# First two pairs of row tiles by eight block products, position by position, in a float32 conv + LoRA kernel

## Chip, core and metric

One NeuronCore of a Trainium2 chip. The metric is the device time of one launch in microseconds (us). Engines: PE (TensorE, matmul), ACT (ScalarE), DVE (VectorE), POOL (GpSimd), SP (SyncE, which here only issues loads). Every engine works through its own queue of instructions in order; semaphores make one wait for another.

## The reference

```
x        (64, 64, 1024)   64 samples, 64 channels, length 1024
v = grouped conv1d(x, weight (64,16,9), 4 groups, pad 4) + cond @ c_weight.T + bias    # per sample, channel
W        (1024, 1024), bias (1024,)                       # of the dense layer, on the last axis
A_eff[b] = sum_n gate[b,n] lora_A[n]   (32, 1024)         # 8 blocks b of 8 samples
B_eff[b] = sum_n gate[b,n] lora_B[n]   (1024, 32)
y = v @ W + bias + (v @ A_eff.T) @ B_eff.T + (v @ A_shared.T) @ B_shared.T
out = x + y
```

All arrays are float32.

## The kernel before

**Tiles.** 64 samples x 64 channels are 4096 rows. A row tile has 128 rows, a pair p has two, and there are 16 pairs. Two pairs share one block b of the LoRA tables.

**Arithmetic.** A float32 operand is split into a high part (cast to float32r by ACT, `hi_of`, L236) and a low part (the difference, on DVE or POOL, `lo_of`, L241); a product is high x high + high x low + low x high, so three matmuls of 128x128 by 128x512 for each of four positions k of a block, twelve for a block product.

**Steps of a pair.** `xload p g` loads a quarter of the pair's input; `xhi`, `xlo` split it; `conv p g` runs six matmuls (L274) into one of two PSUM banks for it; `evac` adds the condition on the way to SBUF (DVE, or ACT in four pieces); `turned` transposes on DVE (L293). Groups 0 and 1 make up the first row tile, 2 and 3 the second. The pair's activations are then a 2x2 block matrix A11, A12, A21, A22 (row tile x half of the inner axis), W is B11, B12, B21, B22.

**Products.** Each pair is multiplied by seven block products (Winograd's form of Strassen's method), with sums of A blocks (`asum`: S1 to S4, on POOL, L316) and of W blocks (`wsum`: T1, T3, N4, T2, L385):

```
PRODUCTS = ((A11, B11, "a"), (A12, B21, "a"), (S1, T1, "d"), (S3, T3, "c"), (A22, N4, "c"), (S2, T2, "b"), (S4, B22, "d"))
```

`prod p j` is product j of pair p (L490). `yhi`, `ylo` split its A operand. `keep` copies an accumulator to SBUF (ACT, L537), `xsum`, `ysum`, `radd`, `yadd` form the sums of products that the method asks for and add them to the residual rows (DVE, some on POOL, L543 to L560). `lora p b` makes the small product with the LoRA A table (L501, L502), `delta` adds the product with the B table and the bias to the accumulators (L566), `total` adds an accumulator to the residual rows (DVE, L572), `store` writes them. Five PSUM banks (`pmm`) serve products, `fmm`, `mix`, `cmul` and separate deltas.

**Weights.** W comes as 16 pieces of 128x512 (`wload k h`, two DMAs each). The shared LoRA is folded into it: `fmm k h` multiplies (L375), `fadd k h` adds the result to the piece (DVE, L379). `whi b k` and `wlo b k` split a piece, in place b for a block or a sum of blocks. All pieces lie in one pool of 57 slots. The gated LoRA tables are made in the kernel: `lload` loads 16 pieces (256 KB each), `mix` multiplies by the gates (L424), `mixout` copies out (ACT), `mixput` writes to DRAM, and per block b `aload`, `ahi`, `adiff`, `alo` and `bload`, `bhi`, `blo` fetch and split what is needed. `saload`, `sahi`, `salo`, `sbload`, `sbhi`, `sblo` do it for the shared tables.

**Order.** A single hand-written string, `ORDER`, names all steps; each step issues its instructions, and at the end dependencies without semaphores fix that order within each engine. A letter v, p or a at a step's end names DVE, POOL or ACT. `busy n` runs n matmuls on constants at the start. Before, the first two pairs interleave products with single positions: `prod p j k 1 alone` is position k of product j, and with alone = 1 it goes to an accumulator of its own ("e"), added by another `total`. Products of pairs 0 and 1 run there in the order 3, 5, 6, 2, 4, 0, 1, each for both pairs, as the sums of W become ready.

Of the kernel before, what the change touches and what calls it, by code (L numbers as in the profile page):

```python
# [15 lines left out]
P = 128  # L16
# [21 lines left out]
A11, A12, S1, S3, A22, S2, S4 = range(7)  # L38
# [3 lines left out]

BLOCKS = ("a", "d", "c", "b")

ORDER = """
warm, twload 0, gload, small 1, busy 26, saload 0, twload 1, small 0, xload 0 0, cwload, ctload, xload 0 1,
xload 0 2, thi 0, xload 0 3, sbload 0, bihi, tlo 0 v, saload 1, sbload 1, bilo, thi 1, wload 4 1, tlo 1 v,
wload 0 1, xhi 0 0, cwide, wload 5 1, xhi 0 1, xlo 0 0 v, cmul, wload 1 1, xlo 0 1 v, conv 0 0, wload 6 1,
csum, wload 2 1, sahi 0, salo 0 p, sbhi 0, conv 0 1, xload 1 2, evac 0 0 v, sahi 1, xload 1 0, sblo 0 v,
xload 1 1, sbhi 1, wload 7 1, turned 0 0, salo 1 p, evac 0 1 a, wload 3 1, sblo 1 v, wload 0 0, xhi 0 2,  # L50
turned 0 1, fmm 4 1, fmm 0 1, xhi 0 3, wload 1 0, fmm 5 1, fadd 0 1, xlo 0 2 p, fmm 1 1, fmm 6 1, wload 2 0,
fadd 4 1, fmm 2 1, wload 3 0, conv 0 2, fadd 6 1, xlo 0 3 p, xload 1 3, fadd 2 1, biput 0, fmm 7 1, biput 1,
fadd 5 1, wsum 3 0 p, evac 0 2 a, fmm 3 1, rload 0 1, conv 0 3, rload 1 1, fadd 1 1, xhi 1 0, turned 0 2,
fmm 0 0, whi 3 0, fmm 1 0, fmm 2 0, xlo 1 0 v, evac 0 3 a, fadd 7 1, wlo 3 0 p, xload 2 0, conv 1 0, xhi 1 1,
turned 0 3, xlo 1 1 v, wsum 3 1 p, lload 0 0, fmm 3 0, xhi 1 2, fadd 1 0, xload 2 1, conv 1 1, evac 1 0 a,
asum 0 3, fadd 0 0, whi 3 1, wload 4 0, fadd 2 0, fmm 4 0, fmm 5 0, yhi 0 3, fadd 3 0, xlo 1 2 p, fmm 6 0,
xhi 1 3, ylo 0 3 v, fmm 7 0, evac 1 1 a, conv 1 2, xlo 1 3 v, wlo 3 1 p, lload 0 1, wload 5 0, fadd 3 1, gmask,
conv 1 3, xhi 2 0, turned 1 0, wsum 3 2 p, wload 6 0, prod 0 3 0 1 0, evac 1 2 v, whi 3 2, wload 7 0,
turned 1 1, xlo 2 0 p, prod 0 3 1 1 0, xhi 2 1, turned 1 2, evac 1 3 a, xload 2 2, conv 2 0, fadd 4 0,
wlo 3 2 p, lload 0 2, wsum 3 3 v, mix 0 0, evac 2 0 a, fadd 6 0, xlo 2 1 p, prod 0 3 2 1 0, fadd 5 0, whi 3 3,  # L60
lload 0 3, xload 2 3, mix 0 1, fadd 7 0, mixout 0 0, wlo 3 3 p, lload 0 4, lload 0 5, conv 2 1, lload 0 6,
xhi 2 2, turned 1 3, lload 0 7, mixout 0 1, lload 1 0, xlo 2 2 v, asum 1 3, lload 1 1, prod 0 3 3 1 0,
mixput 0 0, wsum 2 0 v, evac 2 1 a, mixput 0 1, mix 0 2, lload 1 2, wsum 5 0 v, asum 0 2, xload 3 0, yhi 1 3,
mix 0 3, whi 5 0, lload 1 3, ylo 1 3 v, mix 0 4, keep 0 3, wlo 5 0 v, wsum 2 1 p, mixout 0 3, prod 1 3 0 1 0,
mixout 0 4, mixput 0 3, asum 0 5, wsum 5 1 v, mix 0 5, lload 1 4, mixout 0 2, mixput 0 4, mix 0 6, whi 5 1,
mixput 0 2, asum 0 6, yhi 0 5, wlo 5 1 v, prod 1 3 1 1 0, mixout 0 5, ylo 0 5 v, mix 0 7, yhi 0 6, mixput 0 5,
wsum 2 2 v, asum 1 2, prod 1 3 2 1 0, mixout 0 6, ylo 0 6 v, prod 0 5 0 1 0, mixout 0 7, mixput 0 6,
wsum 5 2 v, lload 1 5, asum 1 5, xhi 2 3, prod 1 3 3 1 0, mixput 0 7, whi 5 2, xlo 2 3 v, prod 0 5 1 1 0,
keep 1 3, asum 1 6, wlo 5 2 v, xload 3 1, conv 2 2, yhi 1 5, wsum 2 3 v, whi 6 0, ylo 1 5 v, wsum 5 3 p,
prod 0 5 2 1 0, yhi 1 6, wlo 6 0 v, lload 1 6, prod 1 5 0 1 0, xhi 3 0, aload 0, ylo 1 6 v, conv 2 3, asum 0 2,  # L70
whi 5 3, xlo 3 0 v, wlo 5 3 v, whi 6 1, xload 3 2, prod 1 5 1 1 0, wlo 6 1 p, xhi 3 1, lload 1 7,
prod 0 5 3 1 0, whi 6 2, xlo 3 1 v, prod 1 5 2 1 0, asum 1 2, wlo 6 2 v, whi 6 3, xload 3 3, keep 0 5,
prod 0 6 0 1 1, wlo 6 3 v, yhi 0 2, prod 1 5 3 1 0, wsum 4 0 v, wsum 4 1 p, whi 2 0, prod 0 6 1 1 1, ylo 0 2 v,
keep 1 5, prod 1 6 0 1 1, wlo 2 0 v, wsum 4 2 p, yhi 1 2, mix 1 0, adiff 0 v, ahi 0, ylo 1 2 v, prod 1 6 1 1 1,
whi 2 1, alo 0 v, mixout 1 0, prod 0 6 2 1 1, wlo 2 1 v, wsum 4 3 p, aload 1, whi 2 2, mixput 1 0, mix 1 1,
wlo 2 2 v, whi 2 3, prod 1 6 2 1 1, mixout 1 1, wlo 2 3 v, lora 0 2, whi 4 0, mixput 1 1, mix 1 2, wlo 4 0 v,
whi 4 1, adiff 1 p, prod 0 6 3 1 1, wlo 4 1 v, whi 4 2, mixout 1 2, prod 1 6 3 1 1, wlo 4 2 v, yhi 0 4,
mixput 1 2, mix 1 3, total 0 1 1, whi 4 3, mix 1 4, total 1 1 1, ylo 0 4 p, yhi 1 4, wlo 4 3 v, whi 0 0,
prod 0 2 0 1 0, ylo 1 4 v, mixout 1 3, lora 0 3, prod 0 2 1 1 0, mixout 1 4, wlo 0 0 v, mixput 1 3, whi 0 1,
mixput 1 4, mix 1 5, turned 2 0, wlo 0 1 v, whi 0 2, prod 1 4 0 1 0, mixout 1 5, turned 2 1, wlo 0 2 p,  # L80
prod 0 2 2 1 0, evac 2 2 a, mixput 1 5, evac 2 3 v, prod 0 4 0 1 0, whi 0 3, turned 2 2, mix 1 6, wlo 0 3 v,
whi 1 0, mix 1 7, mixout 1 6, wlo 1 0 v, prod 0 4 1 1 0, whi 1 1, mixput 1 6, turned 2 3, mixout 1 7,
prod 1 2 0 1 0, wlo 1 1 v, asum 2 2, mixput 1 7, prod 0 4 2 1 0, whi 1 2, prod 1 2 1 1 0, asum 2 3,
prod 0 4 3 1 0, wlo 1 2 v, prod 1 2 2 1 0, whi 1 3, bload 0 0, yhi 0 0, lora 1 2, wlo 1 3 v, prod 1 2 3 1 0,
ylo 0 0 v, bload 0 1, lora 1 3, yhi 1 0, total 1 1, prod 0 0 0 1 0, rload 0 2, ysumd 1, ylo 1 0 p,
prod 0 2 3 1 0, rload 0 3, prod 0 0 1 1 0, yhi 0 1, total 0 1, prod 1 0 0 1 0, bhi 0 0, ylo 0 1 v,
prod 0 0 2 1 0, bhi 0 1, ysumd 0, blo 0 0 p, prod 1 0 1 1 0, total 0 2, prod 0 0 3 1 0, rload 1 2, blo 0 1 v,
yadd 0 p, prod 1 0 2 1 0, xsum 0 5, rload 1 3, lora 0 0, radd 0 1 v, radd 0 2 p, prod 1 0 3 1 0, yhi 1 1,
radd 0 3 v, prod 0 1 0 1 0, ylo 1 1 v, lora 0 1, prod 0 1 1 1 0, xsum 1 5, axlow 0, conv 3 0, yadd 1 v,
radd 1 1 p, axsum 0, radd 1 3 v, axhi 0, prod 0 1 2 1 0, axlo 0, xhi 3 2, prod 1 1 0 1 0, evac 3 0 v,  # L90
prod 0 1 3 1 0, xlo 3 2 v, prod 1 1 1 1 0, yhi 2 0, turned 3 0, xload 4 0, delta 0 1 1, ylo 2 0 v, delta 0 2 1,
delta 0 0 0, lora 1 0, total 0 1 2, prod 1 1 2 1 0, yhi 2 1, total 0 2 2, delta 0 3 1, store 0 1, lora 1 1,
ylo 2 1 v, store 0 2, prod 1 1 3 1 0, ahi 1, total 0 3 2, prod 2 0, axlow 1, alo 1 v, store 0 3, yhi 2 2,
aload 2, ylo 2 2 v, rload 0 0, rload 1 0, lora 2 0, keep 2 0, prod 1 4 1 1 0, axsum 1, yhi 2 3, bload 1 0,
prod 2 1, adiff 2 v, axhi 1, ylo 2 3 v, total 0 0 0, asum 2 5, axlo 1, store 0 0, asum 2 6, prod 1 4 2 1 0,
delta 1 1 1, prod 1 4 3 1 0, total 1 1 2, delta 1 2 1, yhi 2 4, total 1 2, delta 1 3 1, delta 1 0 0, bload 1 1,
lora 2 1, store 1 1, bhi 1 0, total 1 3 2, ylo 2 4 p, conv 3 1, yhi 2 5, radd 1 2 v, store 1 3, total 1 0 0,
blo 1 0 p, prod 2 2, xhi 3 3, total 1 2 2, store 1 0, evac 3 1 a, rload 2 0, xlo 3 3 v, ylo 2 5 p, xload 4 1,
store 1 2, turned 3 1, bhi 1 1, rload 2 2, blo 1 1 v, lora 2 2, rload 2 1, keep 2 2, conv 3 2, rload 2 3,
yhi 2 6, rload 3 0, ylo 2 6 v, prod 2 3, xhi 4 0, evac 3 2 v, xlo 4 0 v, rload 3 2, turned 3 2, xload 4 2,  # L100
conv 3 3, yhi 3 0, keep 2 3, ylo 3 0 v, lora 2 3, ysum 2 v, xhi 4 1, prod 2 4, axlow 2, evac 3 3 v, xlo 4 1 p,
axsum 2, turned 3 3, axhi 2, xload 4 3, axlo 2, asum 3 2, prod 2 5, yhi 3 1, ylo 3 1 v, asum 3 3, delta 2 0,
yhi 3 2, xsum 2, prod 2 6, total 2 0, ylo 3 2 p, radd 2 2 v, store 2 0, radd 2 1 v, radd 2 3 p, delta 2 2,
yhi 3 3, prod 3 0, total 2 2, yadd 2 v, ylo 3 3 p, store 2 2, rload 3 1, asum 3 5, delta 2 1, keep 3 0,
lora 3 0, total 2 1, asum 3 6, delta 2 3, yhi 3 4, conv 4 0, total 2 3, rload 3 3, store 2 1, ylo 3 4 v,
store 2 3, prod 3 1, xhi 4 2, evac 4 0 v, xlo 4 2 v, turned 4 0, xload 5 0, lora 3 1, bload 2 0, conv 4 1,
yhi 3 5, bload 2 1, ylo 3 5 v, prod 3 2, xhi 4 3, evac 4 1 v, xlo 4 3 v, turned 4 1, xload 5 1, lora 3 2,
# [112 lines left out]
def adaln_ffn(ctx: ExitStack, tc: tile.TileContext, xt, x, tw, w0, w1, w2, la, lb, gt,  # L220
# [488 lines left out]
```

## Time and profile before

| | us |
|---|---|
| median of 3 runs | 510.44 (510.01 to 510.85) |
| profiled execution, its own time | 510.2 |
| its span, first to last instruction | 508.2 |
| PE busy | 489.5 (96%) |
| DVE busy | 381.4 (75%) |
| POOL busy | 237.9 (47%) |
| ACT busy | 204.5 (40%) |
| mean granted PE clock | 0.984 |

A busy PE is not PE at its peak: a matmul's record is about 0.4 us long, and the next starts 0.23 us after it. Where work is bound by PE, the distance of starts counts.

### The profile page before, as it was taken

The page shows a single profiled execution, that of the slowest core. Times are in us where ns is not written, and L with a number is a line of the kernel's source. Part 1 is how long each engine was busy: PE and PEld are TensorE (multiplying, and loading weights), DVE is VectorE, ACT ScalarE, POOL GpSimd, SP SyncE. Part 2 cuts the span into 40 slices and gives each one's busy share as a digit, 9 for nine tenths or more (in the row PEclk, how much of TensorE's full clock was granted, in tenths as well). Part 3 has the DMA queues.
Part 4 walks back from the last instruction along what each step waited for, and adds up shares of the span by engine and source line. Part 5 has one row for each costly group of instructions (what it writes and reads, how often), then busy time and mean ns, then how long its engine had stood idle before and what let it go on. Part 6 is the DMA issues. An engine that isn't in the chain of part 4 may idle for free.

```text
span 508.2 us, 6944 instructions
## 1 busy us (share of the span) xinstructions
PE 489.5 (96%) x2386; PEld 383.7 (75%) x2386; DVE 381.4 (75%) x499; ACT 204.5 (40%) x398; POOL 237.9 (47%) x179
## 2 busy tenths in 40 slices
PE   7889799999999999999999999999999999999995
PEld 6643455877888788888888888888888888888884
DVE  3799998887786868677776869576767868686844
ACT  4566557335324342334324342433334342423330
POOL 2587843515443816083534726082625634191611
PEclk9799889999999999999999999999999999999998
DMA  8989332436453442426252533336252633324122
GB/s 227 272 262 316 102 89 57 125 101 193 163 163 87 145 125 83 158 67 213 64 157 72 187 94 125 106 93 188 62 176 54 201 91 127 92 84 144 39 88 83
DMA packets 52114, 66.99 MB, mean 132 GB/s; under 512 B 5872, under 2 KB 33520, under 8 KB 52080
## 3 DMA queue, kind: packets, MB, share of 16 engines
q1 hardware_dynamic: 42800, 49.77, 34.6%
q10 hardware_dynamic: 9216, 16.78, 8.8%
q8 instruction: 19, 0.31, 0.3%
q14 instruction: 15, 0.12, 0.1%
q0 software_dynamic: 64, 0.01, 0.0%
HBM read 47.65 MB, written 18.87 MB: 131 GB/s over the span
## 4 chain that ended last, share of the span: by engine, by line
PE 79%; DVE 7%; DMA 7%; issue 3%; SPq 2%; ACT 1%; ACTq 0%; DVEq 0%
PE mm_c L490 16%; PE mm_d L490 15%; PE mm_a L490 15%; PE cv L274 14%; PE mm_b L490 8%; DMA xt<-in_dram 3%; PE axp L501 3%; PE axp L502 3%; DVE ws L385 1%; DMA sbr<-in_dram 1%; DVE wl L241 1%; DMA wr<-in_dram 1%; PE mx L424 1%; DVE r L556 1%; DVE y L241 1%
## 5 line engine op out<-in xcount | busy, mean ns | idle before, releaser
L241 POOL TENSOR_TENSOR xs<-xt,xs 128x516 fp32r<-128x516 f32 x19 | 25.2, 1331 | 152.4 <-ACT xs L236 152.4
L490 PE MATMUL mm_c<-wh,y 128*128 128x512 f32 x256 | 88.8, 401 | 0.7 <-DVE y L241 0.7
L490 PE MATMUL mm_a<-wh,y 128*128 128x512 f32 x256 | 86.2, 396 | 0.1
L274 PE MATMUL cv<-xs,th 128*128 128x512 f32 x256 | 83.8, 410 | 1.2 <-DVE v L285 1.0
L490 PE MATMUL mm_d<-wh,y 128*128 128x512 f32 x240 | 81.1, 395 | 0.0
L236 ACT CAST y<-s 128x512 fp32r<-128x512 f32 x64 | 39.8, 621 | 93.4 <-PE axp L501 31.8
L241 DVE TENSOR_TENSOR y<-z,y 128x512 fp32r<-128x512 f32 x45 | 47.3, 1050 | 34.0 <-ACT y L236 34.0
L241 DVE TENSOR_TENSOR y<-s,y 128x512 fp32r<-128x512 f32 x45 | 35.7, 794 | 44.1 <-ACT y L236 43.9
L490 PEld LDWEIGHTS mm_c<-wh,y 128*128 128x128 f32 x256 | 48.2, 188 | 16.5 <-issue 4.1
L490 PEld LDWEIGHTS mm_a<-wh,y 128*128 128x128 f32 x256 | 48.3, 188 | 11.5 <-ACT c L537 0.6
L274 PEld LDWEIGHTS cv<-xs,th 128*128 128x128 f32 x256 | 46.8, 193 | 11.4 <-issue 2.2
L236 ACT CAST xs<-xt 128x516 fp32r<-128x516 f32 x64 | 39.9, 626 | 36.9 <-PE cv L274 22.9
L490 PEld LDWEIGHTS mm_d<-wh,y 128*128 128x128 f32 x240 | 45.2, 188 | 11.1 <-issue 0.8
L236 ACT CAST y<-z 128x512 fp32r<-128x512 f32 x48 | 29.8, 621 | 54.0 <-PE mm_c L490 45.1
L490 PE MATMUL mm_a<-wl,y 128*128 128x512 f32 x128 | 50.5, 395 | 0.0
L490 PE MATMUL mm_c<-wl,y 128*128 128x512 f32 x128 | 50.5, 395 | 0.0
L293 DVE STREAM_TRANSPOSE z<-v 128x512 f32<-128x512 f32 x64 | 44.8, 702 | 3.7 <-ACT v L283 3.5
L490 PE MATMUL mm_d<-wl,y 128*128 128x512 f32 x120 | 47.3, 394 | 0.0
L556 DVE TENSOR_TENSOR r<-r,c 128x512 f32<-128x512 f32 x32 | 44.8, 1436 | 0.1
L490 PE MATMUL mm_b<-wh,y 128*128 128x512 f32 x128 | 44.6, 406 | 0.0
L274 PE MATMUL cv<-xs,tl 128*128 128x512 f32 x128 | 41.3, 405 | 0.0
L241 DVE TENSOR_TENSOR xs<-xt,xs 128x516 fp32r<-128x516 f32 x45 | 38.1, 847 | 1.7 <-ACT xs L236 1.6
(108 smaller groups left out, 901.3 us busy)
## 6 DMA issues: line engine op xcount, KB each, us to landing
xt<-in_dram SPq DMA_DIRECT2D x64, 258.0 KB, 2.9
r<-in_dram SPq DMA_DIRECT2D x64, 256.0 KB, 3.4
out_dram<-r ACTq DMA_DIRECT2D x64, 256.0 KB, 2.7
ls<-in_dram SPq DMA_DIRECT2D x16, 256.0 KB, 5.0
br<-eff SPq DMA_DIRECT2D x48, 64.0 KB, 2.4
wr<-in_dram SPq DMA_DIRECT2D x16, 176.0 KB, 4.1
eff<-ls SPq DMA_DIRECT2D x16, 128.0 KB, 2.4
wr<-in_dram SPq DMA_DIRECT2D x16, 80.0 KB, 3.9
```

What stands on the lines that cost most here:

```text
L236: nc.scalar.copy(dst, src)
L241: engs[eng].tensor_tensor(dst, src, f32(hi), ALU.subtract)
L274: nc.tensor.matmul(ps, a[:, kt, g, :], b[:, :, kt:kt + P], start=(n == 0), stop=(n == len(prods) - 1))
L293: nc.vector.transpose(z[:, :, :, :, gg, :], vs.pop((p, g)).rearrange("p m j -> p (m j)"))
L385: engs[eng].tensor_tensor(t, wr[m, k], wr[n, k], ALU.subtract)
L424: nc.tensor.matmul(mps[w, i], gm.rearrange("p b i -> p (b i)"), lraw[w, i], start=True, stop=True)
L490: nc.tensor.matmul(ps, a[:, k, :], b[bb, k], start=s, stop=(k == HK - 1 and q == 2), skip_group_check=not first)
L501: both = lambda **f: nc.tensor.matmul(ps, s[:, k0 + k].rearrange("p q r -> p (q r)"), h[:, k, :], **f)
L502: one = lambda **f: nc.tensor.matmul(ps[0:R], s[:, k0 + k, 0, :], l[:, k, :], **f)
L556: engs[eng].tensor_tensor(r, r, cop[p, "x"], ALU.add)
```

## The change

Pairs 0 and 1 no longer use the seven products. The new step `plain p b k` adds position k (0 to 7, the whole inner axis) to output block b (0 to 3), three matmuls, into one of four accumulators that stay open until the block is complete. These pairs need A21 as an operand and neither sums of A, `keep`, `xsum`, `ysum`, `radd` nor `yadd`; W's block B12 is split as well. From pair 2 on the seven products are used, in nearly the order of before. Further:

- The head of `ORDER` is new: the order of loads, `busy 40` for `busy 26`, W's positions k one after the other (both halves h), the sums of W and their splitting during pairs 0 and 1, LoRA tables at other places.
- `wsum` writes its sum over the block that is no longer needed, where it took a new slot.
- `saload` and `sbload` load one copy of 32 rows in place of three; `sahi`, `sbhi` cast it to two places.
- The first eight `lload`s use slots of other tags (r and s); two `xload`s of pair 1, and A11 and A21 of pair 1, use slots of tag c.
- In later pairs some steps go from POOL to DVE: of 48 `radd`, 16 were on POOL and now none of 42; `xlo` 19 to 9 on POOL, `ylo` 22 to 14, `alo` 6 to 0, `blo` 9 to 0, `adiff` 6 to 1; `evac` on ACT 11 to 5.

```diff
-A11, A12, S1, S3, A22, S2, S4 = range(7)
+A11, A12, S1, S3, A22, S2, S4, A21 = range(8)
+PLAIN = 2
...
-warm, twload 0, gload, small 1, busy 26, saload 0, twload 1, small 0, xload 0 0, cwload, ctload, xload 0 1,
...
+warm, twload 0, small 1, twload 1, busy 40, xload 0 0, xload 0 1, small 0, saload 0, sbload 0, saload 1,
+sbload 1, cwload, bihi, ctload, thi 0, bilo, biput 1, tlo 0 v, thi 1, xload 0 2, xload 0 3, tlo 1 v, wload 0 0,
+xhi 0 0, wload 0 1, xlo 0 0 v, gload, xhi 0 1, xload 1 0, conv 0 0, xload 1 2, sahi 0, xlo 0 1 v, xload 1 3,
+lload 0 0, salo 0 v, conv 0 1, xload 1 1, sbhi 0, cwide, lload 0 1, lload 0 2, sblo 0 v, sahi 1, lload 0 3,
+cmul, lload 0 4, salo 1 v, lload 0 5, fmm 0 0, gmask, xhi 0 2, biput 0, sbhi 1, wload 1 0, wload 1 1, xhi 0 3,
+wload 2 0, wload 2 1, wload 3 0, csum, xlo 0 2 v, lload 0 6, wload 3 1, xlo 0 3 v, evac 0 0 a, evac 0 1 v,
+conv 0 2, wload 4 0, fadd 0 0, sblo 1 p, wload 4 1, turned 0 0, whi 0 0, conv 0 3, lload 0 7, evac 0 2 v,
+xhi 1 0, turned 0 1, fmm 0 1, fmm 1 0, evac 0 3 v, xlo 1 0 p, fmm 1 1, yhi 0 0, xload 2 0, fadd 0 1, conv 1 0,
+turned 0 2, ylo 0 0 p, whi 7 0, turned 0 3, xhi 1 1, xhi 1 2, xlo 1 1 v, yhi 0 7, xlo 1 2 v, xload 2 1,
+conv 1 1, yhi 0 1, wlo 0 0 v, yhi 0 4, wlo 7 0 v, wload 5 0, wload 5 1, plain 0 0 0, ylo 0 1 v, evac 1 0 a,
+wload 6 0, plain 0 1 0, evac 1 1 v, wload 6 1, conv 1 2, ylo 0 7 v, wsum 2 0 v, plain 0 2 0, turned 1 0,
+evac 1 2 v, ylo 0 4 p, fadd 1 0, turned 1 2, plain 0 3 0, whi 0 1, fadd 1 1, turned 1 1, fmm 2 0, whi 7 1,
+wlo 0 1 p, fadd 2 0, yhi 1 0, plain 0 2 1, wlo 7 1 v, wload 7 0, wload 7 1, whi 0 2, fmm 2 1, plain 0 0 1,
...
     def yhi(p, b):
-        t = slot("y", f"y{b}_{p}", (P, 2, HK, P), F32R)
-        spl[p, b] = (t[:, 0], t[:, 1])
+        if p == 1 and b in (A11, A21):
+            spl[p, b] = [slot("c", f"y{q}{b}_{p}", (P, HK, P), F32R) for q in "hl"]
+        else:
+            t = slot("y", f"y{b}_{p}", (P, 2, HK, P), F32R)
+            spl[p, b] = (t[:, 0], t[:, 1])
...
     def wsum(b, k, eng="p"):
-        t = wr[b, k] = piece(f"ws{b}_{k}")
-        m, n = {T1: (B12, B11), T3: (B22, B12), T2: (B22, T1), N4: (B21, T2)}[b]
+        m, n, to = {T1: (B12, B11, B11), T3: (B22, B12, B12), T2: (B22, T1, B22), N4: (B21, T2, B21)}[b]
+        t = wr[to, k]
         engs[eng].tensor_tensor(t, wr[m, k], wr[n, k], ALU.subtract)
+        wr[b, k] = t
...
+    def plain(p, b, k):
+        hf, h = divmod(b, 2)
+        kh, kk = divmod(k, HK)
+        if k == 0:
+            acc[p, BLOCKS[b]] = pmm.tile([P, HN], F32, tag="mm", name=f"mm{p}_{BLOCKS[b]}")
+        yh, yl = spl[p, ((A11, A12), (A21, A22))[hf][kh]]
+        w = HOME[kh, h], kk
+        for q, (m, n) in enumerate(((yh, wh[w]), (yh, wl[w]), (yl, wh[w]))):
+            nc.tensor.matmul(acc[p, BLOCKS[b]], m[:, kk, :], n, start=(k == 0 and q == 0), stop=(k == 7 and q == 2))
...
     def lora(p, b):
         hf, blk, k0 = ((0, A11, 0), (0, A12, HK), (1, S1, 0), (1, A22, 2 * HK))[b]
+        if p < PLAIN and hf:
+            blk, k0 = ((A21, 0), (A22, HK))[b - 2]
```

## The prediction

> **What bounds the kernel now.** I read the page first, then busy time by stage, then the chain of waits in order of time, and last the timelines of TensorE (PE) and VectorE (DVE) where a stage showed idle time.
>
> ```profile
> span 508.2 us, 6944 instructions
> PE 489.5 (96%) x2386; PEld 383.7 (75%) x2386; DVE 381.4 (75%) x499; ACT 204.5 (40%) x398; POOL 237.9 (47%) x179
> ...
> 0.00:25.40 25.40, 20.18 (x79) 16.86 (x80) 14.91 (x24) 12.89 (x29) 10.61 (x14) 0.87 0.89 250
> 25.40:50.80 25.40, 22.91 (x72) 11.12 (x71) 23.83 (x30) 16.86 (x42) 20.62 (x17) 1.00 0.94 289
> 50.80:76.20 25.40, 20.90 (x71) 13.35 (x69) 24.73 (x25) 14.33 (x28) 16.49 (x11) 0.87 0.34 95
> 203.00:305.00 102.00, 102.00 (x525) 83.22 (x524) 73.72 (x102) 38.88 (x72) 45.32 (x36) 1.00 0.41 127
> ```
>
> A stage row gives length, then busy time (and count) of PE, weight loads, DVE, ACT and POOL, then PE's granted clock, DMA share and GB/s. After 203 us PE is never idle: only less PE work helps there. From 25 to 76 us DVE is busy 48.6 of 50.8 us, and PE issues 143 matmuls where the later rate (525 in 102 us) would give 261. The start is bound by DVE, the rest by PE.
>
> The chain of waits prices a matmul and a pair:
>
> ```profile
> 287.32 2.79 PE mm_a L490 x12
> ...
> 315.56 2.79 PE mm_a L490 x12
> ```
>
> Twelve matmuls take 2.79 us, 0.2325 each; the same product of two neighbouring pairs lies 28.24 us apart. **The budget:** 16 pairs x 28.23 = 451.7; 16 mix steps at 1.0 = 16.0; 16 fmm at 0.23 = 3.7; cmul 1.1; together 472.5 of 508.2. Of the 35.7 us left, 5.3 lie behind PE's last matmul (from 502.9 on) and 0.4 in two later periods of 28.48 and 28.35. So **the head's gap is 30.0 us**: time in the first 110 us in which PE did none of this work, or did it at half clock. When the first product starts (31.6 us) 16.2 us are done (eight convs at 1.42, all fmm, cmul): 15.4 of the gap lie before it, 14.6 behind. What the second part looks like:
>
> ```profile
> 54.64 1.76 DVE L241 TENSOR_TENSOR wl<-ws,wh 128x512 fp32r<-128x512 f32 x1
> 56.33 0.68 DVE L385 TENSOR_TENSOR ws<-wr,wr 128x512 f32<-128x512 f32 x1
> ...
> 54.24 1.61 POOL L316 TENSOR_TENSOR s<-z,s 128x512 f32<-128x512 f32 x1
> ...
> 56.46 0.50 PE L490 MATMUL mm_b<-wl,y 128*128 128x512 f32 x1 [2.03 <-DVE wl L241]
> ...
> 64.44 0.51 PE L490 MATMUL mm_b<-wl,y 128*128 128x512 f32 x1 [2.41 <-DVE wl L241]
> ```
>
> PE waits for the low half of a W piece. The DVE instruction that makes it takes 1.76 us beside a POOL instruction, and its like takes 0.68 when POOL is idle (56.33). Each such meeting costs DVE 1.07 us, and POOL is busy 37 of those 50.8 us.
>
> **The change, part by part.** *PE work.* Pairs 0 and 1 run 8 products of 12 matmuls instead of 7: 24 more matmuls x 0.2325 = **+5.6 us**, all on PE, the bounding engine; nothing hides them. conv, lora, delta, fmm and mix are as many as before. *So the head's gap has to fall from 30.0 below 24.4 for a gain.* I walk the new order along its queues with the trace's durations.
>
> *Up to the first product.* ACT: bihi now stands first and its load is in at 4.8 us (that cast's start in the trace), then two thi and xhi 0 0 at 0.62: 6.85. DVE follows with tlo, tlo, xlo, xlo at 0.69, to 8.7. The 40 warm-up matmuls (26 took 5.9 us at half clock; 14 more at full clock are 1.6) end at 8.7 too, where the first conv starts now as well (8.65). Then conv, conv, cmul: 12.6. gmask's mask takes the slot that cmul's operand held, so DVE goes on at 12.6 with gmask 0.95, csum 0.42 and 15 instructions at 0.69 (xlo, evac, turned, fadd, the first wlo): the last but one ends at 23.6, and plain 0 0 0 starts at about 24.0, 7.6 us earlier than a product does now. But only six convs, four fmm and cmul are done then, 10.5 us: **a gap of 13.5**, against 15.4. The earlier start alone is worth 1.9 us. sahi and sbhi become two casts each (4 x 0.62 more on ACT, before 14 us) and shift nothing that DVE doesn't already wait for.
>
> *Two additions to it.* POOL still runs sblo, xlo 1 0 and ylo 0 0 here; one meeting with a two-input DVE instruction, at the 1.07 above, most likely not all on the path (0 to 2.1): +0.7. And the clock: after the stages with gaps of 2.03 and 2.41 us PE was granted half:
>
> ```profile
> 54.80:58.20 3.40, 1.74 (x6) 1.16 (x7) 3.40 (x4) 1.68 (x4) 2.17 (x2) 1.00 0.62 178
> 58.30:61.60 3.30, 3.30 (x9) 2.53 (x8) 3.30 (x3) 2.17 (x4) 3.30 (x3) 0.50 0.03 11
> ```
>
> The Trainium skill (TensorE: Matmul & The Clock Gate, section "HAM oscillation — how this bites in real kernels") gives as its rule that only PE gaps over about 3.4 us lose the clock. The new order has a gap of 2.15 us here (cmul's end to the next conv, 12.6 to 14.75). By the rule it costs nothing; by the row, 3.4 us at half clock, which makes two convs and the DVE steps behind them 1.1 us later. The row decides that it can happen; its busy share was 51% and here I expect 60 to 70%, so I take +0.5.
>
> *Pair 0 (24 to about 72 us).* PE has 43.7 us of work from plain 0 0 0 to plain 0 1 7, DVE 60 instructions, at 0.69 41.4 us: nearly equal queues, each waiting for the other. All four accumulators stay open for the whole pair, so one PSUM bank of five is left for twelve fmm (returned by fadd on DVE) and eight mix steps (returned by mixout on ACT, 0.58). Walked step by step: plain 0 3 0 waits 0.7 for fadd 1 0, fmm 2 0 another 0.7 for fadd 1 1, the other 19 returns 0.15 each: **+4.3**. POOL has 8 instructions here (20.6 us busy in the like stage before, about 12 now); three of them (wlo 1 1, wsum 3 1, wsum 3 2) fall where DVE is the later queue; at 0.68 each between none and 1.07: **+2.0** (0 to 3.2).
>
> *Pair 1 and the passage to pair 2.* DVE needs 33 us, PE 41; the sixteen T pieces are split here, off the path. bload 0 0 follows the last mixput on SP, and 8.5 us pass from mix 1 7 to blo (mixout 0.6, landing 2.4, three issues and a landing 3.5, cast and difference 1.3, queues), against 9.6 us of PE work before the first delta. No row shows this order; the stage before at 101.6 to 127 was idle 1.05 of 25.4. Bounds 0 and 5, taken **+1.5**.
>
> *SP.* The six lloads put ahead of W, and biput 1, delay W: row 1 of W lands after 5.6 MB, at 250 to 289 GB/s by 23 us, and is needed at 28; row 7 after 9.8 MB at 39, needed at 62. Covered; without the cover, 1.5 MB are 5.5 us. The las and lbs loads shrink by 0.5 MB. The mixputs stand ahead of xload 2 2 on SP with slack of several us. *ACT:* 4 more whi, 6 fewer yhi, 4 fewer keep, free.
>
> *The steady pairs.* radd, xlo, alo, blo go from POOL to DVE, about 3 per pair x 0.69 = +2.1 on DVE, less the meetings saved; DVE now 73.72/102 x 28.23 = 20.4 us per pair, then about 22, under PE's 28.2: 0. Without that cover it would be 1 us in each of 12 pairs. Below nothing is excluded, PE is never idle there. The tail's order on PE is unchanged: 0.
>
> *Sum.* New gap 13.5 + 0.7 + 0.5 + 4.3 + 2.0 + 1.5 = 22.5. Change: 22.5 - 30.0 + 5.6 = **-1.9 us**. The profiled execution took 510.2 (span 508.2): 508.3; it lies 0.24 under the median of 510.44, so **508.5**.
>
> **The rivals.** *The spare bank decides (slower).* Each of the twelve fmm waits until fadd has emptied the one bank, and fadd stands in DVE's queue. If one instruction more is ahead of it than I walked, each return costs 0.5 us more and the gap grows by 6: 514.5. From 0.16 us more per return (1.9/12) the gain is gone. For it: DVE and PE queues of equal length, and PE's waits in the trace end on DVE. Against it: fadd reads PSUM and took 0.68 us (mean) even in the crowded stage.
>
> *The head runs freely (faster).* Fewer POOL instructions let DVE lead everywhere, as from 76 to 101 us, where PE was never idle: half of the 9.0 us behind the 13.5 vanish: 504.
>
> *The steady pairs leak (slower).* DVE at 78% with strict order; 0.4 us of PE wait per pair x 12 = 4.8: 513.3. Against it: 0.4 us in all of two periods is all that PE loses there now, with DVE at 72%.
>
> *The change does not do what it says:* the first product starts early only by putting convs behind it; if it comes at 28 us with the same 10.5 us done, 4 us are lost: 512.5.
>
> **How the numbers follow.** The walk holds (506 to 511): 0.44, of which 0.30 under 509.4 (0.2%, about what a measurement of this kernel can tell from no change), 0.12 within, 0.02 above. Head free: 0.18, all faster. Spare bank: 0.20, steady leak 0.08, late first product 0.10, all slower but 0.04 within. So faster 0.48, same 0.16, slower 0.36. The range 503.5 to 516 takes in the free head and the bank's full price; the likeliest case alone is 506 to 511.
>
> **What would show it.** Right: first plain matmul near 24 us; PE pieces of pair 0 done near 73; PE busy 24 us or more of 25.4 from 50 to 76; wl waits of 2 us gone; period still 28.23. Wrong: waits of PE for fadd (L379's successor) summing over 5 us; half clock behind 30 us; DVE instructions of 1.7 us before a wait of PE; a period over 28.5.

## The result, and the profile after

| | before | after |
|---|---|---|
| median, us | 509.88 (508.50 to 510.85, 12 runs) | 510.44 (508.74 to 511.64, 12 runs) |
| ratio to before, 95% interval | | 1.0013 (0.9999 to 1.0027) |
| profiled execution / its span | 510.2 / 508.2 | 511.51 / 509.7 |
| mean clock of the profiled execution | 0.984 | 0.992 |

No difference from before is shown: the interval takes in 1. (The 510.44 us in the table of the kernel before was the median of the first three of its runs.) The page of after, and busy time by stage (length, then PE, weight loads, DVE, ACT, POOL, PE's clock, DMA share, GB/s):

```profile
span 509.7 us, 6905 instructions
PE 495.4 (97%) x2424; PEld 386.5 (76%) x2424; DVE 364.1 (71%) x561; ACT 198.0 (39%) x372; POOL 124.9 (24%) x97
...
0.00:25.40 25.40, 19.75 (x88) 16.91 (x89) 15.37 (x27) 15.40 (x29) 6.04 (x12) 0.93 0.85 242
25.40:50.80 25.40, 22.69 (x76) 13.52 (x75) 20.81 (x31) 10.35 (x21) 4.47 (x3) 0.93 0.53 156
50.80:76.20 25.40, 25.34 (x88) 14.40 (x88) 21.31 (x31) 12.65 (x27) 7.37 (x6) 1.00 0.70 202
76.20:101.60 25.40, 25.40 (x131) 15.95 (x131) 18.49 (x32) 14.58 (x29) 1.20 (x1) 1.00 0.34 78
101.60:127.00 25.40, 24.77 (x129) 19.85 (x128) 18.14 (x30) 10.06 (x22) 7.25 (x6) 1.00 0.54 164
203.00:305.00 102.00, 102.00 (x522) 82.74 (x521) 75.70 (x115) 37.46 (x68) 25.83 (x19) 1.00 0.42 125
```

Much of what the change is about did happen. POOL's busy time is half of before (124.9 for 237.9). DVE is busy 17 us less although it runs 62 instructions more, because fewer of them meet one of POOL. From 50.8 to 76.2 us PE was busy 20.90 us before, at a clock of 0.87; now 25.34, at 1.00. What did not go is the stage from 25.4 to 50.8: PE 22.69 of 25.4, at 0.93.

I use the prediction's measure, the gap: start of a matmul less the work at full pitch that PE has behind it. The trace of before, counted matmul by matmul, gives 15.7 at the first product and 30.2 at the first product of pair 2.

| after, at | start, us | gap, us | the gap grew by | predicted |
|---|---|---|---|---|
| first product | 25.47 | 15.13 | | 14.7 |
| first product of pair 1 | 77.22 | 23.40 | 8.27 | 6.3 |
| first product of pair 2 | 123.56 | 26.10 | 2.70 | 1.5 |
| end of PE | 504.40 | 30.44 | 4.34 | |

Before, the gap at PE's end (502.86) is 34.48. So the gap fell by 4.04, the work grew by 5.58, and PE ends 1.54 us later, as the two spans say. (Behind the first product of pair 2 both kernels lose 4.3 us: the later pairs cost nothing more than before.) The medians are only 0.56 apart: each trace is one execution, and that of after (511.51) lies 1.07 above its median, that of before (510.2) 0.32 above. What is to be explained is why the head fell by 4 us and not by the 7.5 of the prediction.

The two places where the trace of after differs most from the walk, first PE, then DVE and POOL, then two stages with their clock:

```profile
16.79 0.80 PE L273 MATMUL cv<-xs,th 128*128 128x512 f32 x2 [4.02 <-ACT v L282]
...
32.02 0.50 PE L493 MATMUL mm_b<-wh,y 128*128 128x512 f32 x1 [2.12 <-DVE wr L383]
```
```profile
14.36 0.86 DVE L417 TENSOR_TENSOR gm<-gg,mask 128x64 f32<-128x64 f32 x1 [1.40 <-DMA gg<-in_dram]
...
26.37 1.78 DVE L240 TENSOR_TENSOR y<-z,y 128x512 fp32r<-128x512 f32 x1
28.07 0.68 DVE L284 TENSOR_TENSOR v<-cv,cadd 128x512 f32<-128x512 f32 x1
28.67 0.68 DVE L240 TENSOR_TENSOR y<-z,y 128x512 fp32r<-128x512 f32 x1
...
26.07 1.52 POOL L240 TENSOR_TENSOR y<-z,y 128x512 fp32r<-128x512 f32 x1 [3.40 <-ACT y L235]
```
```profile
25.40:32.10 6.70, 4.38 (x18) 2.59 (x16) 6.60 (x10) 1.74 (x7) 1.52 (x1) 1.00 0.95 284
...
34.40:37.70 3.30, 3.30 (x9) 2.59 (x8) 2.52 (x5) 1.26 (x3) 0.00 (x0) 0.50 0.85 246
```

*The first.* conv 0 2 waits 4.02 us for a PSUM bank. evac 0 0 on ACT empties it, and it needs csum's sum, which needs gm, which waits for the gates: `gload` now stands in SP's queue behind `biput 1`, two quarters of the input and the first two pieces of W. Behind this wait PE ran at half clock from 17.3 to 20.7.

*The second.* `plain 0 3 0` opens the fourth accumulator in the bank that fmm 1 0 used, and waits until fadd 1 0 (L383) has emptied it. In the 6.7 us before, DVE is idle for 0.10: ahead of the fadd stand four steps that pair 0 doesn't need yet (evac 1 1, wsum 2 0, turned 1 0, evac 1 2), and a split that pair 0 does need (ylo 0 1) takes 1.78 us beside a POOL instruction. 2.4 us behind that wait PE runs at half clock again, from 34.4 to 37.7.

### The profile page after: what moved, and what is told of

The parts are those of the page before. It is cut to its first block, busy times and chain, and to the rows that moved or that the text cites. A ratio compares the mean times of both kernels' runs of the same rounds, so it can differ in the third digit from the quotient of the medians.

```text
span 509.7 us, 6905 instructions
## 1 busy us (share of the span) xinstructions
PE 495.4 (97%) x2424; PEld 386.5 (76%) x2424; DVE 364.1 (71%) x561; ACT 198.0 (39%) x372; POOL 124.9 (24%) x97
## 4 chain that ended last, share of the span: by engine, by line
PE 90%; DMA 4%; DVE 2%; issue 1%; SPq 1%; POOL 1%; DVEq 0%; POOLq 0%
PE cv L273 16%; PE mm_a L505 15%; PE mm_d L505 15%; PE mm_c L505 15%; PE mm_b L505 8%; PE mx L430 3%; PE axp L518 3%; PE axp L519 3%; PE mm_d L493 2%; DMA xt<-in_dram 2%; PE mm_c L493 2%; PE mm_a L493 2%; PE mm_b L493 1%; DMA ls<-in_dram 1%; DVE wl L240 1%
## 5 line engine op out<-in xcount | busy, mean ns | idle before, releaser
L505 PE MATMUL mm_a<-wh,y 128*128 128x512 f32 x224 | 75.0, 396 | 0.0
L505 PE MATMUL mm_c<-wh,y 128*128 128x512 f32 x224 | 74.9, 395 | 0.0
L240 POOL TENSOR_TENSOR y<-z,y 128x512 fp32r<-128x512 f32 x13 | 17.1, 1315 | 137.6 <-ACT y L235 137.6
L505 PEld LDWEIGHTS mm_a<-wh,y 128*128 128x128 f32 x224 | 42.0, 188 | 10.4 <-ACT c L554 0.2
L317 POOL TENSOR_TENSOR s<-s,z 128x512 f32<-128x512 f32 x14 | 21.2, 1514 | 104.0 <-DVE y L240 104.0
L284 DVE TENSOR_TENSOR v<-cv,cadd 128x512 f32<-128x512 f32 x59 | 40.6, 688 | 8.0 <-PE cv L273 5.6
L505 PE MATMUL mm_a<-wl,y 128*128 128x512 f32 x112 | 44.2, 395 | 0.0
L273 PE MATMUL cv<-xs,tl 128*128 128x512 f32 x128 | 41.4, 406 | 0.0
L240 DVE TENSOR_TENSOR y<-z,y 128x512 fp32r<-128x512 f32 x35 | 35.6, 1017 | 5.5 <-ACT y L235 4.2
L518 PE MATMUL axp<-y,sta 128*64 128x128 f32 x248 | 37.9, 222 | 0.5 <-DVE axs L533 0.5
L505 PE MATMUL mm_b<-wh,y 128*128 128x512 f32 x112 | 38.1, 401 | 0.0
```

What stands on the lines that cost most here:

```text
L240: engs[eng].tensor_tensor(dst, src, f32(hi), ALU.subtract)
L273: nc.tensor.matmul(ps, a[:, kt, g, :], b[:, :, kt:kt + P], start=(n == 0), stop=(n == len(prods) - 1))
L284: nc.vector.tensor_tensor(v, ps, c.unsqueeze(2).to_broadcast([P, 4, P]), ALU.add)
L317: engs[eng].tensor_tensor(t, m, n, op)
L505: nc.tensor.matmul(ps, a[:, k, :], b[bb, k], start=s, stop=(k == HK - 1 and q == 2), skip_group_check=not first)
L518: both = lambda **f: nc.tensor.matmul(ps, s[:, k0 + k].rearrange("p q r -> p (q r)"), h[:, k, :], **f)
```

## The experiments

Four theories of where the expected gain went: *two late steps* (gload, fadd 1 0), each mended by itself; *DVE's queue*, whose order holds back what pair 0 needs; *loads of W* that come late behind the LoRA tables; and *the clock*, that each short idle time of PE is paid a second time at half clock. A fifth: *the later pairs* lose what the head gains. Medians and ratios to before (which ran with each set on the same chip, medians 509.66 to 509.90, mean clock 0.988; the sets ran on different chips, so across sets it is the ratios that compare). Only fadds earlier, the two deferred kernels and the last one have intervals that don't meet after's:

| kernel | median, us (runs) | ratio to before (95%) | mean clock |
|---|---|---|---|
| after | 510.44 (12) | 1.0013 (0.9999 to 1.0027) | 0.992 |
| gload earlier | 510.83 (22) | 1.0029 (1.0016 to 1.0042) | 0.990 |
| fadds earlier | 512.50 (8) | 1.0058 (1.0035 to 1.0080) | 0.990 |
| pair 0 short | 509.97 (20) | 1.0006 (0.9995 to 1.0017) | 0.988 |
| pair 1 short | 509.41 (20) | 0.9998 (0.9982 to 1.0013) | 0.990 |
| steps deferred | 512.83 (6) | 1.0066 (1.0047 to 1.0084) | 0.988 |
| deferred, tables later | 513.53 (6) | 1.0073 (1.0051 to 1.0095) | 0.989 |
| gload earlier, fill | 509.28 (22) | 0.9994 (0.9983 to 1.0005) | 0.995 |
| before's later pairs | 511.07 (22) | 1.0023 (1.0010 to 1.0036) | 0.991 |
| before, filled | 511.51 (15) | 1.0029 (1.0017 to 1.0041) | 0.989 |
| fill alone | 509.84 (22) | 1.0002 (0.9986 to 1.0017) | 0.994 |
| two fills | 511.29 (15) | 1.0044 (1.0025 to 1.0062) | 0.993 |
| **fills, deferred anew** | **506.75 (5)** | **0.9943 (0.9930 to 0.9955)** | 0.998 |

### gload earlier

```diff
-... bilo, biput 1, ... xlo 0 0 v, gload, xhi 0 1, ...
+... bilo, gload, biput 1, ... xlo 0 0 v, xhi 0 1, ...
```

> The changed kernel with one load moved: the small gate table (gload) is issued ahead of biput 1, where SP stands idle, and no longer behind the first two pieces of W. Theory A (single late steps in in-order queues make the gap): DVE's 1.4 us wait for that table goes, csum, evac 0 0 and conv 0 2 come 1.4 us earlier, PE's wait of 4.0 us at 16.8 us falls to about 2.6, the half clock behind it may go too; the first product starts near 24 us, the span is 1.4 to 2.5 us shorter: 508 to 509, ratio to the kernel before about 0.997 to 0.999. Theory B (the supply of split W pieces by DVE, which works without a break from 15 to 38 us, sets the pace): the wait only moves to the next fadd, under 0.5 us gained, ratio 1.001.

The first product came at 24.01, 1.46 us earlier, and the profiled span was 2.0 us shorter than after's (507.7). The median is not: 510.83, over runs from 508.8 to 513.3. PE's rows of this kernel at the wait:

```profile
15.56 0.74 PE L274 MATMUL cv<-xs,th 128*128 128x512 f32 x2 [2.95 <-ACT v L283]
...
16.60 1.63 PE L274 MATMUL cv<-xs,th 128*128 128x512 f32 x4
```

The bank wait is 2.95 for 4.02, and half clock follows all the same (16.9 to 20.3; four matmuls in 1.63 us, where full clock takes 1.1). Over the 22 runs time and mean clock go against each other (correlation -0.85): much of what a run takes goes with how often the clock is lost.

How much of the 1.46 us is gload's? Six profiled kernels have after's steps unchanged up to the first product. In five of them (after, fadds earlier, pair 0 short, pair 1 short, steps deferred) gm waits 0.98 to 1.43 us for the gates, and the first product comes at 25.47 to 26.40. In the sixth, before's later pairs, the same steps go differently:

```profile
13.04 0.23 DVE L417 TENSOR_TENSOR gm<-gg,mask 128x64 f32<-128x64 f32 x1
...
15.45 0.74 PE L273 MATMUL cv<-xs,th 128*128 128x512 f32 x2 [2.54 <-ACT v L282]
...
22.93 0.39 PE L493 MATMUL mm_a<-wh,y 128*128 128x512 f32 x1
```

There SP issues gload at 10.28 us (after: 11.21), the gates are in time, the bank wait is 2.54 us, no half clock follows until 31.3, and the first product comes at 22.93. So the order lets the gates be late, but one execution with that order starts earlier than every one with gload moved (23.32 to 24.01). A difference of one or two microseconds at the first product between two traces is not by itself the effect of an edit.

### fadds earlier

```diff
-plain 0 1 0, evac 1 1 v, ... ylo 0 7 v, wsum 2 0 v, plain 0 2 0, ... ylo 0 4 p, fadd 1 0, turned 1 2, plain 0 3 0, whi 0 1, fadd 1 1, ...
+plain 0 1 0, fadd 1 0, evac 1 1 v, ... ylo 0 7 v, fadd 1 1, wsum 2 0 v, plain 0 2 0, ... ylo 0 4 p, turned 1 2, plain 0 3 0, whi 0 1, ...
```

> The changed kernel with fadd 1 0 moved ahead of evac 1 1 and fadd 1 1 ahead of wsum 2 0 in DVE's queue. Theory A (the one spare PSUM bank): plain 0 3 0 no longer waits 2.1 us for fadd 1 0, fmm 2 0 follows at once, and the half clock from 34.4 to 37.7 us that follows this wait goes: 2.2 us and up to 1.7 us, so 506.5 to 508.5, ratio 0.995 to 0.998. Theory B (DVE's supply sets the pace): what DVE does earlier here, it does later elsewhere; the wait moves to ylo 0 7 and wlo 7 1, under 0.8 us gained, ratio 1.000.

PE's next wait in its trace:

```profile
35.61 0.50 PE L379 MATMUL pf<-sb,sa 96*128 96x512 f32 x1 [2.90 <-DVE wr L383]
```

The wait of 2.12 us before plain 0 3 0 is gone (0.74 us stand one step before it), and 2.90 us stand later, at fmm 2 1, for the next fadd: the steps that the two fadds overtook are now ahead of fadd 2 0. The gap at the third position is 21.81 for 20.70 (0.6 of it was there at the first product), the median 512.5. So that one wait, taken away, gains nothing. A queue in which DVE has no idle time only shows the same lateness at another step.

### pair 0 short, pair 1 short

```diff
-    nc.tensor.matmul(acc[p, BLOCKS[b]], m[:, kk, :], n, start=...)
+    c = P if p == 0 and q == 2 else HN          # p == 1 in the other kernel
+    nc.tensor.matmul(acc[p, BLOCKS[b]][:, 0:c], m[:, kk, :], n[:, 0:c], start=...)
```

> The changed kernel with the third matmul of each of pair 0's 32 plain steps cut to 128 of its 512 columns (that part of the low x high term is left out). Every wait and all work of the other engines stay. It takes 32 x 0.172 = 5.5 us of work from PE, as much as the 24 matmuls that the change adds. Theory A (PE's own queue with short waits): most of it comes back, 4 to 5.5 us, ratio 0.990 to 0.993. Theory B (pair 0 is bound by DVE and the spare bank): PE only waits longer, under 2.5 us come back, ratio over 0.996.

> The same cut in pair 1 (the third matmul of its 32 plain steps over 128 of 512 columns; that part of the low x high term is left out). Both theories: pair 1 is bound by PE, so 5 to 5.5 us come back, ratio 0.990 to 0.992. If less than 4 us come back, the passage to pair 2 (LoRA B table, splitting of the T pieces) is a bound that my prediction had off the path.

The third matmul of each of a pair's 32 positions covers 128 of 512 columns. That was meant to take away 5.5 us of PE work, what the change adds; where PE is never idle (pair 1 up to 103 us) the trace gains 0.15 us per position, so it is about 4.8 (an estimate: 32 x 0.15). Medians lie 0.5 us (pair 0) and 1.0 us (pair 1) under after's, with intervals that overlap its own. In the profile of the first, pair 0 is 2.7 us shorter, so nearly half of the removed work is lost again within the pair; and its runs have a mean clock of 0.988 for 0.992, by estimate some 1.6 us of PE's time (0.0032 x 508). In the second the time follows PE's work as far as 103 us, 3.2 us gained; then PE waits 2.88 us in the passage to pair 2, for the B table of the gated LoRA and for DVE's other LoRA steps, where after waits 0.63, and 2.0 us are left at pair 2:

```profile
104.34 0.50 PE L579 MATMUL dl<-bst,axt 98*128 98x512 f32 x1 [0.82 <-DVE bst L240]
...
114.19 0.24 PE L519 MATMUL axp<-y,sta 128*64 128x128 f32 x1 [1.24 <-DVE axs L534]
...
116.44 0.47 PE L579 MATMUL mm_d<-bst,axt 98*128 98x512 f32 x1 [0.82 <-DVE axt L542]
```

So PE's work alone does not set the end of either pair. In pair 0 DVE's chain runs almost level with PE; in pair 1 the LoRA steps stand close behind PE and become the limit when PE's work shrinks.

### steps deferred; deferred, tables later

```diff
-evac 1 1 v, ... turned 1 0, evac 1 2 v, ... turned 1 2, ... turned 1 1, ... yhi 1 0, ... ylo 1 0 v, ...
+(these seven behind "fadd 3 1"; "wsum 2 0 v" behind "wsum 2 1 v")
```
```diff
+(the second kernel also: lload 0 0 to lload 0 5 behind "wload 3 1")
```

> The changed kernel with DVE relieved between 26 and 38 us: evac, turned of pair 1's first three groups and the split of its A11 stand behind fadd 3 1, wsum 2 0 behind wsum 2 1, so eight DVE instructions (about 5 us) leave the stretch in which DVE has no idle time and go to 38 to 50 us, where it is idle a third of the time. Theory B (DVE's supply of split W pieces sets the pace up to 38 us): positions 1 to 3 of pair 0 start 3 to 4 us earlier, the wait of 2.1 us and the half clock behind it go, and 2 to 4 us come back: ratio to the kernel before 0.994 to 0.998. Theory C (the loads of W set the pace there, DMA share 0.95 to 1.01): fadd then waits for the loads, under 1 us comes back, ratio 1.000 to 1.002.

> As e5_defer, and the first six lloads (1.5 MB) behind wload 3 1 instead of ahead of wload 1 0. Theory B: W's loads are not late, so as e5_defer within 0.5 us, or slower if mix 0 0 then waits. Theory C: W's positions 1 to 3 land 5 us earlier and with DVE free the gain of 3 to 5 us shows here and not in e5_defer: ratio 0.992 to 0.995.

Positions 1 and 2 did come earlier: the third position starts at 35.48 for 38.71, with a gap of 17.46 for 20.70. Then it was lost again. PE and ACT of the first of the two kernels, and the stage behind:

```profile
41.73 0.50 PE L379 MATMUL pf<-sb,sa 96*128 96x512 f32 x1 [1.86 <-ACT ls L435]
```
```profile
40.06 0.62 ACT L235 CAST yh<-z 128x512 fp32r<-128x512 f32 x1 [3.74 <-DVE z L292]
...
41.11 0.57 ACT L435 COPY ls<-mx 64x512 f32<-64x512 f32 x1
```
```profile
42.60:49.40 6.80, 6.13 (x11) 3.27 (x12) 2.41 (x5) 2.24 (x4) 0.00 (x0) 0.50 0.09 20
```

yhi 1 0 stands in ACT's queue ahead of mixout 0 0 (L435) and waits 3.74 us for the transposes that were put off. mixout returns the spare PSUM bank, so fmm 4 0 waits 1.86 us, and 6.8 us at half clock follow. The deferral moved the block from DVE's queue to ACT's. With the tables behind the first pieces of W the trace is the same (third position at 35.90): loads of W are not the bound.

### The clock: fills

A fill is `busy n`: n matmuls on constants, whose result nobody reads. It changes no other step.

```diff
-cmul, lload 0 4, salo 1 v, lload 0 5, fmm 0 0, gmask, ...
+cmul, lload 0 4, salo 1 v, lload 0 5, fmm 0 0, busy 22, gmask, ...
```

> The changed kernel with gload ahead of biput 1 (as in e1_gload) and 22 warm-up matmuls of 0.116 us behind fmm 0 0, which fill PE's wait for conv 0 2. Theory D (the clock gate makes the head slow, and the run's place against its windows makes the spread): the half clock at 17 us goes in nearly every run, conv 0 2 and 0 3 take 1.42 us each, DVE no longer waits for them (0.8 us twice); mean clock about 0.003 higher than e1_gload's 0.9895 and 1.5 to 2 us less than it: 509, ratio 0.999. Theory B: the head follows DVE's queue and gains only the two waits, at most 0.8 us: 510, ratio 1.001; the clock rises all the same.

> The kernel of after with 22 matmuls on constants behind the first fmm, the loads' order as in after. Clock theory: no half clock at 17 us, median about 509.3, as the kernel that also moves gload (509.28): the fill and not gload made that one faster. Rival (gload and fill both needed): about 510.4, as after.

With gload moved, PE's rows at the place shown above:

```profile
12.24 2.79 PE L610 MATMUL idle<-axt 98*128 98x256 f32 x22
16.47 0.73 PE L274 MATMUL cv<-xs,th 128*128 128x512 f32 x2 [1.44 <-ACT v L283]
...
17.51 1.10 PE L274 MATMUL cv<-xs,th 128*128 128x512 f32 x4
```

conv 0 2 starts 0.9 us later than without the fill (16.47 for 15.56), yet the four matmuls of the last row take 1.10 us for 1.63, no half clock stands here (the next is at 32.2), and the first product comes at 23.63 for 24.01. The median is 1.55 us lower than that of the same kernel without the fill, and the two intervals (0.9983 to 1.0005, 1.0016 to 1.0042) don't meet; the mean clock of the runs is 0.995 for 0.990. The fill does nothing else, so the clock is a cost of its own. With the fill alone and gload where after has it, the median is 509.84: between after and the last, and apart from neither.

It is no remedy that works anywhere, as two kernels show. The first puts 26 such matmuls into the gap of before between conv 0 1 and the first fmm:

> The kernel of before with 26 matmuls on constants put into PE's own early gap (11.7 to 15.1 us, the wait for the low half of the LoRA B table), nothing else. Clock theory: if an idle PE of some 3 us is what loses the clock behind it, the profiled head runs at full clock from 15 to 21 us (6.8 us at half clock in the profile of before, 3.4 us of work lost at most) and the median falls by 1 to 2 us, to about 508.5, mean clock above 0.99; the filled kernel of after (509.28) is then no better than a filled before. Rival (the head is bound by DVE, not by PE's clock): half clock goes, the median stays within 0.2% of before, because DVE sets the pace behind 15 us.

```profile
13.83 3.27 PE L597 MATMUL idle<-axt 98*128 98x256 f32 x26
16.94 1.91 PE L375 MATMUL pf<-sb,sa 96*128 96x512 f32 x6
```

Here the half clock fell on the first convs (8.8 to 12.2, ahead of the fill and so not its doing), conv 0 1 ended later, and the fill kept PE until 16.9, 1.8 us behind the start that fmm has in before (15.10). The first product came 2.0 us late, half clock came back at 29.3 and at 63.4, and the median is 511.51. The second puts 12 into accumulator b ahead of plain 0 3 0:

> As the kernel with gload moved ahead and 22 matmuls behind the first fmm (509.28), and 12 more matmuls on constants into accumulator b just before its first position (the place where PE waits 2.1 us for the sum on DVE); the first position overwrites them. Clock theory: the half clock at 32 us goes as well, 1.7 us of PE work regained, of which DVE's queue takes a part: median 508 to 509. Rival (DVE sets the pace there, the clock is only an effect of the wait): 509.3, unchanged.

```profile
30.06 1.69 PE L492 MATMUL mm_b<-axt 98*128 98x256 f32 x12 [2.11 <-DVE wr L384]
31.58 0.41 PE L496 MATMUL mm_b<-wh,y 128*128 128x512 f32 x1
```

The edit misses its aim: accumulator b is the bank that fadd 1 0 returns, so the fill itself waits 2.11 us, then takes 1.5 us on the path. It doesn't test the clock at this place; it only shows that a fill behind the wait costs its length.

### before's later pairs

```diff
-(from prod 6 0 on: after's steps)
+(from prod 6 0 on: before's steps, in its order and on its engines)
```

> The changed kernel up to the first product of pair 6, and from there on the steps in the order and on the engines of the kernel before (radd, xlo, ylo partly on POOL again). If the moves from POOL to DVE in the steady pairs cost nothing, as predicted, the time is that of the changed kernel within 0.3 us, ratio 1.0013. If the steady pairs leak: their distance in the trace falls from 28.28 to 28.235 us, 0.4 us over ten pairs, ratio 1.0005; a larger leak would show as more than 1 us.

511.07, nothing gained, in spite of the early start of its profiled execution. With the equal gap behind 123 us, the moves from POOL to DVE are free in the later pairs. Two rows of after's chain of waits say it, with starts 28.28 us apart for 28.24 before:

```profile
175.29 2.80 PE mm_a L505 x12
...
203.57 2.80 PE mm_a L505 x12
```

### fills, deferred anew

```diff
-... fmm 0 0, gmask, ... evac 1 1 v, ... turned 1 0, evac 1 2 v, ... turned 1 2, ... turned 1 1, ... yhi 1 0, ... ylo 1 0 v, ...
+... fmm 0 0, busy 22, gmask, ... wsum 2 3 v, evac 1 1 v, turned 1 0, evac 1 2 v, turned 1 1, turned 1 2, whi 1 0, ...
+... wlo 6 0 v, yhi 1 0, ylo 1 0 v, ...     (and: gload ahead of biput 1; wsum 2 0 behind wsum 2 1;
+ 8 fill matmuls ahead of plain 0 3 0)
```

> As the last, with 8 matmuls in place of 12 there, and the five steps that prepare pair 1 (evac 1 1, turned 1 0, evac 1 2, turned 1 1, turned 1 2) behind wsum 2 3, yhi 1 0 and ylo 1 0 behind wlo 6 0, wsum 2 0 behind wsum 2 1: DVE's steps that pair 0 does not need go where DVE has idle time (behind 40 us). If the order of DVE's queue is what pair 0 loses 8.3 us to, positions 1 and 2 come 3 us earlier as in the first deferral, ACT's mixout is no longer held, and the gap at the end of pair 0 falls by 2 to 3 us; median 507 to 508, the fastest. If DVE's total work or the passage to pair 2 takes it back, 509 to 510.

506.75 us, 0.9943 of before (0.9930 to 0.9955), and under every other kernel here. Stages, PE and DVE of this kernel:

```profile
25.40:32.10 6.70, 6.61 (x32) 4.99 (x31) 4.95 (x8) 2.46 (x4) 1.32 (x2) 1.00 0.96 274
...
25.40:50.80 25.40, 24.47 (x89) 13.78 (x87) 22.63 (x35) 10.65 (x18) 2.98 (x3) 1.00 0.64 184
```
```profile
27.23 1.21 PE L492 MATMUL mm_b<-axt 98*128 98x256 f32 x8
28.28 0.39 PE L496 MATMUL mm_b<-wh,y 128*128 128x512 f32 x1
```
```profile
24.20 2.38 DVE L241 TENSOR_TENSOR y<-z,y 128x512 fp32r<-128x512 f32 x2
26.50 1.27 DVE L384 TENSOR_TENSOR wr<-wr,pf 128x512 f32<-128x512 f32 x2
...
29.42 0.69 DVE L384 TENSOR_TENSOR wr<-wr,pf 128x512 f32<-128x512 f32 x1 [1.64 <-PE pf L380]
```

The two fadds follow directly on the low halves of A; plain 0 3 0 starts at 28.28 for 32.02 and waits for nothing. From 25.4 to 32.1 PE is busy 6.61 us for 4.38 (1.2 of it fill), and DVE, not PE, is the one that waits (1.64 us, for fmm). No half clock stands between the warm-up and the tail. The gap:

| at | after | this kernel |
|---|---|---|
| first product | 15.13 | 12.98 |
| third position of pair 0 | 20.70 | 14.82 |
| first product of pair 1 | 23.40 | 18.25 |
| first product of pair 2 | 26.10 | 21.09 |

At the third position it is 5.9 us less: 2.15 on the way to the first product, which before's later pairs shows can also come without these edits, and 3.7 from positions 0 and 1, of which 1.7 are the half clock from 34.4 to 37.8 and 2.1 the wait for fadd 1 0, both gone, with 1.05 us of fill in their place. Of the 5.9 us 0.9 is given back later; pair 1 with its passage costs 2.8 (2.7 in after), as before. Put into the prediction's sum: 21.1 - 30.2 + 5.6 = -3.5; measured against before -3.15. The five runs lie within 0.8 us at clocks from 0.997 to 0.999. How much belongs to the deferral and how much to the 8 fill matmuls was not separated; against "gload earlier, fill" both together are worth 2.5 us, and the trace of that kernel has one window of half clock (32.2 to 35.6, 1.7 us of work) that this one has not. The 8 matmuls take 0.94 us of PE in which plain 0 3 0 could have run (its fadd ended at 27.1), so the same order without them may be up to that much faster; this was not tried.

## Why the prediction was right or wrong

The time, 510.44, lies inside the range and at the upper end of the walk's own range of 506 to 511, in the part called "within". The gain of 1.9 us that it took as likeliest did not come (measured +0.56); no change had a chance of 0.16. Of its signs of being right, 25.34 us busy from 50 to 76, no wait for wl over 0.1 us in pair 0 and a period of 28.28 came; the end of pair 0 (77 for 73) did not. Of its signs of being wrong two came: half clock behind 30 us, and a DVE instruction of 1.78 us ahead of a wait of PE. The waits for fadd sum to 2.4 us, not over 5. The mechanism was as predicted: less meeting of DVE and POOL, an earlier first product that is worth less than its time because fewer convs are done, 5.58 us more PE work. Sizes in the sum were off, nearly all one way:

- **"plain 0 0 0 starts at about 24.0, a gap of 13.5", +0.7 and +0.5.** 25.47 and 15.13, for 24.0 and 14.7: the total is near, its parts are not. The walk had a wait of 2.15 us at conv 0 2 and DVE going on with gmask at 12.6. It missed that gload is behind other loads on SP: gm waits 1.40 us for the gates, and the bank wait becomes 4.02. It also took 4.8 us, from the trace of before, for bihi's cast, which comes at 5.46 in after. Both vary: with the same steps, before's later pairs has that cast at 4.79, no wait for the gates, a bank wait of 2.54 and the first product at 22.93, so the walk's 24.0 lies between single executions. An error the other way helped it there: it priced DVE's steps at 0.69 us, the length of a record, but back to back they start 0.61 us apart (mean of 231 in after; 28.07 and 28.67 above), which over its 15 steps is about 1.2 us (an estimate, 15 x 0.08). The place of gload in SP's queue was not counted; what it costs in the median is not shown ("gload earlier": 510.83).
- **"By the rule it costs nothing; by the row, 3.4 us at half clock."** The row was right in kind and undersized at +0.5. In after half clock follows a wait of 4.02, which the Trainium skill's rule (TensorE: Matmul & The Clock Gate, "HAM oscillation — how this bites in real kernels") covers too. But it also follows waits of 2.95 ("gload earlier") and 2.12 (after, at 32 us), both under the rule's 3.4 us, and none follows the wait of 2.54 in "before's later pairs": the length of the wait alone does not decide it. The fill shows that it is worth 1.5 us of the median.
- **Pair 0: "plain 0 3 0 waits 0.7 ... the other 19 returns 0.15 each: +4.3", and +2.0 for POOL.** 8.27 for 6.3. From the first product to the first matmul of pair 0's second position that follows fmm 2 0 (33.54) 3.65 us are lost, of them 2.12 in the wait called 0.7; then 1.92, the half clock from 34.4 on; then only 2.70 over the rest of the pair. So the price was not spread over 21 returns: it lies in the first 13 us, DVE hardly idles in the first 9 of them (0.10 us from 25.4 to 32.1), and from 38 us on DVE has idle time (5.59 us busy of 8.2 from 37.8 to 46.0). In the 2.70 us hardly a wait is long enough to show as idle time. "Nearly equal queues" does not hold over the whole pair: 60 DVE steps at 0.61 are 36.6 us and not 41.4, and with the slowed ones DVE was busy 43.0 of the pair's 51.75 us, PE 49.0. It is the first quarter in which DVE is the later queue.
- **Pair 1 and the passage, +1.5.** 2.70, well inside its bounds of 0 and 5. In after it is not the passage: PE is never idle from 76 to 101.6, and its waits from 98 to 124 sum to 0.63 us, none of them for the B table. The rest are delays too short to show as idle time, left unexplained. The tables are off the path in after, but close to it: "pair 1 short" stops gaining at 103 us and waits there.
- **"+5.6 us, all on PE; nothing hides them."** As an amount right (5.58). As a price it is in doubt: taking some 4.8 us away returns 2.7 us within pair 0 and 2.0 within pair 1 in the traces, and in the medians 0.5 and 1.0, not clear of noise. Work and gap were added as if independent; where DVE or the tables run level with PE, PE work taken out turns into waiting.
- **Steady pairs 0, tail 0.** Right, and by the experiment too.

The rivals: *the spare bank* is real, but as one wait of 2.12 us, not as 0.5 us on each of twelve returns; with the same banks the last kernel doesn't have it, so it hangs on DVE's order and not on the number of banks alone. *Head runs freely* didn't happen in after; the last kernel, with DVE's steps in another order, goes part of the way (506.75; the rival's price was 504). *Steady leak* and *late first product* (28 us) didn't happen.

## What to carry to other kernels

Ask of a queue without idle time which of its steps the bound engine needs next, and put the others where the queue has idle time; moving the one step that the trace names only moves the wait. When a step is put off, follow its successor in every other in-order queue: it blocks what stands behind it there. An idle time of two or three microseconds on PE may be paid twice, the second time as half clock, so look at the granted clock in the stage behind a wait before you price the wait.

## What the runs showed of the hardware

In these traces half clock comes in windows of 3.4 us or 6.8 us, each 3.4 us worth 1.7 us of work. In after and the kernels made from it, every PE wait of 1.9 to 2.9 us that ended between 29 and 43 us has one near its end (beginning from 0.2 us before it to 2.4 behind it; the last kernel has no such wait). At 15 to 17 us it also came with waits of 3.0 to 4.6 us, but not with one of 2.54. In before it came with waits of 3.4, 2.0 and 2.4 us. The same steps had it from 17.3 to 20.7, from 15.3 to 22.1 or not at all, so its place varies from execution to execution. It makes part of the spread: time and mean clock correlate at -0.3 to -0.4 in before, -0.43 in after, and between -0.36 and -0.97 in eleven of the changed kernels. The one kernel without such a window in its profile spreads over 0.8 us (5 runs), the others over 2 to 6. A DVE instruction with two SBUF operands took 1.78 us beside a POOL instruction, and its like 0.68 without, as in before.
